# A graph network on one core: the seam of layers 1 and 2, and the last two steps of layer 3, put together anew

## The chip, the cores and the metric

The kernel runs on one core of a Trainium2 chip. The metric is the time of one execution on the device in microseconds (us); three runs of the kernel before gave 2731.63, 2735.09 and 2736.67, median 2735.09. The engines are TensorE (PE; its weight loads are PEld), VectorE (DVE), ScalarE (ACT), GpSimd (POOL) and SyncE (SP), which here only issues DMAs.

## The reference, cut to what matters

Four layers over a graph of N = 4096 nodes with 256 features, all in float32. Each is a residual step with a layer norm behind it:

```python
x = ln(x + attention(x, adj))                    # layer 0: 4 heads, mask adj == 0
x = ln(x + softmax(leaky(es + ed), adj > 0) @ (x @ W1))   # layer 1
d = adj.sum(1) ** -0.5                            # 0 where the sum is 0 (layer 2)
x = ln(x + ((d[:, None] * adj * d[None, :]) @ x) @ W2.T + b2)   # layer 2
x = ln(x + relu((d[:, None] * adj * d[None, :]) @ x @ W3))      # layer 3
```

The change touches the end of layer 1, the start of layer 2, and the end of layer 3, the end of the kernel.

## The kernel before

`xc` holds the rows of x in on-chip memory: 32 chunks of 128 rows. `wh`, a view of the tile `store`, holds layer 1's projected features.

Layer 1 works on 32 units (one chunk of output rows each) in four steps each; `gat_step(t)` runs a pipeline in which the products `attend` (L805) of a step stand six steps behind its scores. Unit u's masks `mk1` (L731) are loaded by SP into buffers of the pool `bias` (`bp`, seven buffers of 4 KB per partition). `finish` (L815, L817, and `ln_stats`, L115 and L116) adds the unit's result onto its chunk and takes mean and variance. The last unit's `finish` waits for the last products of layer 1.

Layers 2 and 3 multiply by the adjacency matrix in the seven-product scheme of Strassen: the matrix is cut in 2 x 2 parts of rows and columns, and the features in 2 x 2 parts as well. One layer is four blocks `jb` of 512 columns in each half, one block 16 steps `c`, so 64 steps a layer and 128 in all (`t`, `n_all`). A step multiplies a pair of chunks p and p + 16:

- `load(t)` (L943): two DMAs of 512 KB from `adjT` into a tile `a`, three steps ahead; four tiles in the pool `l2adj`.
- `sums(t)` (L952, L953, L954): DVE forms five sums and differences of the four parts of `a` into `asum` (two buffers), one step ahead.
- `prepare(p, layer)`: DVE normalizes the two chunks (L124), ACT scales them into `y` (L919; `y` lies in `store`, which layer 1 has left by then), POOL adds the bias `b2` to the chunk in layer 2 (L923), and DVE forms five sums `ysum` (L925, L928, L931). In layer 2's first block the pair p = c + 2 is prepared at the end of step c.
- `Block.product(i, t)` (L983): product i of seven, in the order 0 to 6, added up over the 16 steps in a PSUM bank `m{i}` of its own. Products 2 and 3 take a part of `a` itself as their right side, the other five a part of `asum`.
- after a block, `keep` (L989 on ACT, L991 on DVE) copies the seven banks to `e`; `combine` (L999 to L1008, on DVE) forms the block's four results `hT`; `rows(n)` multiplies them by the weights (L1017, eight row chunks of two halves f each, into the bank `y`) and adds them to `xc` (layer 2: L1026; layer 3: L1031 relu on ACT, then L1032 on DVE) with `ln_stats`. `at_step` spreads this over the steps of the next block, between its products. `block_rstd` (L909 to L911) turns the variances of eight chunks into factors, and `store(h)` normalizes four chunks (L124) and writes them to `out` with one DMA of 512 KB (L1040).

The order on every engine is that of the program (`tc.manual_schedule()`). At the seam it reads:

```python
ln_rstd(0, NCH)            # all 32 chunks: L119 to L121
for t in range(3):
    load(t)
with tc.manual_schedule():
    prepare(0, 0)
    sums(0)
    prepare(1, 0)
```

Behind the last step nothing is left to lie beside: `keep`, then for each half `combine` and four `rows`, then `block_rstd`, then both `store`.

Of the kernel before, what the change touches and what calls it, by code (L numbers as in the profile page):

```python
# [8 lines left out]
F32 = mybir.dt.float32  # L9
BF16 = mybir.dt.bfloat16  # L10
AF = mybir.ActivationFunctionType
# [5 lines left out]
P = 128  # L17
# [27 lines left out]
def tile_gnn(  # L45
# [52 lines left out]
    es_q = keep.tile([P, NA, NBK], F32, name="es_q")  # L98
    pick = keep.tile([P, NA, NA, QB], F32, name="pick")
    ed_b = keep.tile([P, QK], F32, name="ed_b")  # L100
    mid = ExitStack()
    bp = mid.enter_context(tc.tile_pool(name="bias", bufs=7))
    zp = mid.enter_context(tc.tile_pool(name="z", bufs=13))
    ps_q = mid.enter_context(tc.tile_pool(name="ps_q", bufs=1, space=PSUM))
    sc = [ps_q.tile([P, TS], F32, name=f"sc{j}") for j in range(2)]
# [14 lines left out]
        nc.scalar.activation(rstd[:, c0:c1], rstd[:, c0:c1], AF.Sqrt)  # L120
        nc.vector.reciprocal(rstd[:, c0:c1], rstd[:, c0:c1])  # L121

    def ln_apply(dst, src, ci):
        nc.vector.tensor_scalar(  # L124
            dst, src, mv[:, ci, 0:1], rstd[:, ci : ci + 1], ALU.subtract, ALU.mult
        )

# [582 lines left out]

    with ExitStack() as l1:
# [145 lines left out]
        with tc.manual_schedule():  # L861
            for t in range(n_t + NSB + 8):
                gat_step(t)
                if t + 2 < NJ:
                    project_w(t + 2)
                if t + 3 == NJ:
                    take_es(2 * NSB, NBK)
                    spread_es(2 * NSB, NBK, ps_o.tile([P, 512], F32, tag="pm", name="pe"))

                    for j in range(NJ):  # L870
                        nc.sync.dma_start(
                            xc.rearrange("p (a j) e -> p a j e", j=NJ)[:, :, j, :],
                            x0.rearrange("(a j p) e -> p a j e", p=P, j=NJ)[:, :, j, :],
                        )
                    nc.vector.reciprocal(d3, d3)
                    nc.vector.reciprocal(d2, d2)
                    nc.vector.tensor_scalar(sel, sel, -1.0, 1.0, ALU.mult, ALU.add)
                    nc.vector.tensor_tensor(d2, d2, sel, ALU.mult)
# [3 lines left out]

    with ExitStack() as l2:
        big = l2.enter_context(tc.tile_pool(name="l2big", bufs=1))
        ap_ = l2.enter_context(tc.tile_pool(name="l2adj", bufs=4))
        sp_ = l2.enter_context(tc.tile_pool(name="l2sum", bufs=2))
        wk = l2.enter_context(tc.tile_pool(name="l2work", bufs=3))
        ps_m = l2.enter_context(tc.tile_pool(name="l2ps_m", bufs=1, space=PSUM))

        w2_sb = big.tile([P, 2, D], F32, name="w2_sb")  # L890
        nc.scalar.dma_start(w2_sb, w2T.rearrange("(c p) e -> p c e", p=P))
        b2_b = big.tile([P, D], F32, name="b2_b")
        nc.scalar.dma_start(b2_b, b2.partition_broadcast(P))
        w3_sb = big.tile([P, 2, D], F32, name="w3_sb")
        nc.scalar.dma_start(w3_sb, w3.rearrange("(c p) e -> p c e", p=P))

        NP = NCH // 2
        NJB = N // 2 // BJ
        NSJ = BJ // P
        T1 = NJB * NP  # L900
        y = store[:, 0 : 2 * NP * D].rearrange("p (h c e) -> p h c e", h=2, c=NP)
        ysum = big.tile([P, NP, 5, P], F32, name="ysum")
        mv2 = mv.rearrange("p (h c) k -> p h c k", h=2)
        rstd2 = rstd.rearrange("p (h c) -> p h c", h=2)

# [4 lines left out]
            nc.scalar.activation(r, r, AF.Sqrt)  # L910
            nc.vector.reciprocal(r, r)  # L911

        def prepare(p, layer):

            dv = d2 if layer == 0 else d3
            for h in range(2):
                ci = h * NP + p
                ln_apply(xc[:, ci, :], xc[:, ci, :], ci)
                nc.scalar.activation(  # L919
                    y[:, h, p, :], xc[:, ci, :], AF.Copy, scale=dv[:, ci : ci + 1]  # L920
                )
                if layer == 0:
                    nc.gpsimd.tensor_tensor(xc[:, ci, :], xc[:, ci, :], b2_b, ALU.add)  # L923
            s = ysum[:, p, :, :]
            nc.vector.tensor_tensor(  # L925
                s[:, 1:3, :].rearrange("p a d -> p (a d)"), y[:, 0, p, :], y[:, 1, p, :], ALU.subtract
            )
            nc.vector.tensor_tensor(  # L928
                s[:, 3:5, :], y[:, :, p, 0:P], y[:, :, p, P : 2 * P], ALU.add
            )  # L930
            nc.vector.tensor_tensor(  # L931
                s[:, 0, :], y[:, 0, p, 0:P], y[:, 1, p, P : 2 * P], ALU.add
            )

        adj_t = {}
        adj_s = {}

        def load(t):
            jb, c = divmod(t % T1, NP)
            a = ap_.tile([P, 2, 2, BJ], F32, tag="adj", name="a")  # L940
            for k in range(2):
                m0 = (k * NP + c) * P
                nc.sync.dma_start(  # L943
                    a[:, k, :, :],
                    adjT[m0 : m0 + P, :].rearrange("p (h j i) -> p h j i", h=2, i=BJ)[:, :, jb, :],
                )
            adj_t[t] = a

        def sums(t):
            a = adj_t[t]  # L950
            s = sp_.tile([P, 5, BJ], F32, tag="asum", name="asum")
            nc.vector.tensor_tensor(s[:, 4, :], a[:, 0, 0, :], a[:, 1, 1, :], ALU.add)  # L952
            nc.vector.tensor_tensor(s[:, 0:2, :], a[:, 0, :, :], a[:, 1, :, :], ALU.add)  # L953
            nc.vector.tensor_tensor(s[:, 2:4, :], a[:, :, 0, :], a[:, :, 1, :], ALU.subtract)  # L954
            adj_s[t] = s

        class Block:
            def __init__(self, layer, jb):
# [2 lines left out]

            def product(self, i, t):
                c = t % NP
                a, s = adj_t[t], adj_s[t]
                left = (
                    ysum[:, c, 0, :],
                    y[:, 0, c, 0:P],
                    ysum[:, c, 2, :],
                    ysum[:, c, 1, :],
                    y[:, 1, c, P : 2 * P],  # L970
                    ysum[:, c, 3, :],
                    ysum[:, c, 4, :],
                )[i]
                right = (
                    s[:, 4, :],
                    s[:, 1, :],
                    a[:, 0, 0, :],
                    a[:, 1, 1, :],
                    s[:, 0, :],
                    s[:, 2, :],  # L980
                    s[:, 3, :],
                )[i]
                nc.tensor.matmul(self.m[i], left, right, start=(c == 0), stop=(c == NP - 1))  # L983

            def keep(self):
                self.e = wk.tile([P, 7, BJ], F32, tag="e", name="e", bufs=1)
                for i in range(7):
                    if i % 2 == 0:
                        nc.scalar.copy(self.e[:, i, :], self.m[i])  # L989
                    else:  # L990
                        nc.vector.tensor_copy(self.e[:, i, :], self.m[i])  # L991
# [15 lines left out]
                    tt(o, o, e[2], ALU.add)  # L1007
                    tt(o, o, e[5], ALU.subtract)  # L1008

            def rows(self, n, tag="y"):  # L1010

                h, s = divmod(n, NSJ)
                ci = h * NP + self.jb * NSJ + s
                w = w2_sb if self.layer == 0 else w3_sb
                py = ps_m.tile([P, 512], F32, tag=tag, name="py")
                for f in range(2):
                    nc.tensor.matmul(  # L1017
                        py[:, 0:D],
                        self.hT[:, h, f, s * P : (s + 1) * P],
                        w[:, f, :],  # L1020
                        start=(f == 0),
                        stop=(f == 1),
                    )
                row = xc[:, ci, :]
                if self.layer == 0:
                    nc.vector.scalar_tensor_tensor(  # L1026
# [2 lines left out]
                else:  # L1029
                    r = wk.tile([P, D], F32, tag="relu", name="relu")  # L1030
                    nc.scalar.activation(r, py[:, 0:D], AF.Relu, scale=d3[:, ci : ci + 1])  # L1031
                    nc.vector.tensor_tensor(row, row, r, ALU.add)  # L1032
                ln_stats(wk, row, ci)

            def store(self, h):
                ob = wk.tile([P, NSJ, D], F32, tag="ob", name="ob", bufs=2)
# [14 lines left out]
                f(*args)  # L1051

        n_all = 2 * T1
        ln_rstd(0, NCH)
        for t in range(3):
            load(t)
        with tc.manual_schedule():
            prepare(0, 0)
            sums(0)
            prepare(1, 0)  # L1060
            blk = None
            for t in range(n_all):
                layer, tl = divmod(t, T1)
                jb, c = divmod(tl, NP)
                if c == 0:
                    blk = Block(layer, jb)
                if t + 3 < n_all:
                    load(t + 3)
                if t + 1 < n_all:
                    sums(t + 1)  # L1070
                for i in range(7):
                    blk.product(i, t)
                    if i == 2:
                        do(t, "mid")
                del adj_t[t], adj_s[t]
                if layer == 0 and jb == 0 and c + 2 < NP:
                    prepare(c + 2, 0)
                do(t, "end")
                if c == NP - 1:
                    blk.keep()  # L1080
                    if t == n_all - 1:
                        break
                    at_step(t + 1, "mid", blk.combine, 0)
                    at_step(t + 2, "mid", blk.combine, 1)
                    for n in range(2 * NSJ):
# [8 lines left out]
                    if layer == 1:  # L1094
                        for h in range(2):
                            at_step(t + 3 + NSJ + h, "end", blk.store, h)
            for h in range(2):
                blk.combine(h)
                for n in range(h * NSJ, (h + 1) * NSJ):
                    blk.rows(n, f"m{n % 7}")  # L1100
            block_rstd(NJB - 1)
            for h in range(2):
                blk.store(h)


# [49 lines left out]
```

## Time and profile before

| | us |
|---|---|
| runs: lowest, median, highest | 2731.63, 2735.09, 2736.67 |
| the profiled execution, its span | 2734.35, 2732.6 |
| layer 1's last product ends | 1875.29 |
| layer 2's first product starts | 1881.54 |
| layer 3's last seven-product step starts, ends | 2699.2, 2705.2 |
| PE's last product ends | 2723.0 |

The span is counted from the first to the last instruction; the profiled execution's own time is 1.75 us longer. The mean granted clock of TensorE over the span is 0.992 of full speed. A line such as `L983 PE` names the line of the kernel and the engine; in the chain of waits a row holds its start, its length and what ran or was waited for.

### The profile page before, as it was taken

The numbers are of one execution on the slowest core, as the hardware profiler recorded it, in microseconds if no ns is written. First come the engines' busy times: TensorE is split into PE (matmuls) and PEld (weight loads), VectorE is DVE, ScalarE is ACT, GpSimd is POOL, SyncE is SP. The second block draws the span as 40 slices with busy tenths as digits, with TensorE's granted clock in tenths as the row PEclk, the third lists the DMA queues.
The fourth block names the chain that finished last, engine by engine and source line by source line (L and its number), as shares of the span: only waits on it lengthen the run. The fifth ranks groups of instructions, "written<-read, shape, count | busy, mean of one in ns | idle before, by whom it ended". The sixth has DMA issues, their size and how long they took to land.

```text
span 2732.6 us, 58953 instructions
## 1 busy us (share of the span) xinstructions
PE 2677.8 (98%) x23824; PEld 1836.4 (67%) x23824; DVE 2183.5 (80%) x3995; ACT 1647.8 (60%) x2675; POOL 379.4 (14%) x660
## 2 busy tenths in 40 slices
PE   8999999999999999999979999999999999999997
PEld 4777777777777777777768888885444444444443
DVE  4999999999999989999758888885866577676575
ACT  2899999999999999999857777771100001000000
POOL 1222232222222222223200000001200000000000
PEclk9999999999999999999999999999999999999998
DMA  6444444444444444444452222204554554555552
GB/s 146 94 96 96 89 94 95 92 96 94 88 96 95 92 90 96 97 89 91 143 160 73 77 78 77 74 20 133 179 159 155 174 159 153 168 175 161 183 174 69
DMA packets 679489, 312.35 MB, mean 114 GB/s; under 512 B 553520, under 2 KB 583600, under 8 KB 679216
## 3 DMA queue, kind: packets, MB, share of 16 engines
q1 hardware_dynamic: 655776, 265.10, 39.5%
q0 software_dynamic: 21632, 42.05, 4.3%
q8 instruction: 186, 3.05, 0.5%
q10 hardware_dynamic: 1808, 1.44, 0.2%
q14 instruction: 87, 0.71, 0.1%
HBM read 262.41 MB, written 46.07 MB: 113 GB/s over the span
## 4 chain that ended last, share of the span: by engine, by line
PE 94%; DVE 2%; DMA 2%; issue 1%; ACT 1%; SPq 0%; POOL 0%; DVEq 0%; POOLq 0%; ACTq 0%
PE m L983 28%; PE po L431 17%; PE sc L374 16%; PE po L805 16%; PE ptr L413 11%; PE py L1017 2%; PE pp L343 1%; PE pq L321 1%; PE pv L232 1%; PE pk L212 1%; DMA xt<-in_xT 0%; DMA mk<-edge 0%; DMA norm<-lt 0%; DMA x<-xs 0%; SPq L731 0%
## 5 line engine op out<-in xcount | busy, mean ns | idle before, releaser
L383 DVE CUSTOM_DVE_ANT_0 z<-sc,bias 128x1024 f32<-128x1024 f32 x512 | 606.0, 1221 | 50.9 <-PE sc L374 50.8
L399 ACT ACTIVATE z<-z,nm 128x1024 f32<-128x1024 f32 x512 | 590.6, 1154 | 0.0
L421 ACT COPY pt<-ptr 128x1024 f32<-128x1024 f32 x507 | 510.3, 1007 | 66.5 <-PE ptr L413 65.4
L431 PE MATMUL po<-pt,xc 128*64 128x128 f32 x8192 | 504.0, 276 | 0.0
L374 PE MATMUL sc<-store,qT 64*128 64x512 f32 x2048 | 502.9, 604 | 0.1
L805 PE MATMUL po<-store,pt 128*128 128x257 f32 x2048 | 447.2, 380 | 12.6 <-issue 12.6
L431 PEld LDWEIGHTS po<-pt,xc 128*64 128x64 f32 x8192 | 442.1, 137 | 17.5 <-DVE pt L419 0.2
L413 PEld LDWEIGHTS ptr<-ident,z 64*128 64x128 f32 x8192 | 322.9, 138 | 181.0 <-issue 86.9
L805 PEld LDWEIGHTS po<-store,pt 128*128 128x128 f32 x2048 | 389.1, 190 | 70.5 <-issue 12.7
L983 PE MATMUL m<-asum,ysum 128*128 128x512 f32 x768 | 356.7, 594 | 6.3 <-issue 6.3
L413 PE MATMUL ptr<-ident,z 64*128 64x64 f32 x8192 | 356.7, 225 | 5.1 <-ACT pt L421 3.7
L374 PEld LDWEIGHTS sc<-store,qT 64*128 64x128 f32 x2048 | 193.9, 189 | 115.6 <-issue 109.5
L983 PEld LDWEIGHTS m<-asum,ysum 128*128 128x128 f32 x768 | 146.2, 191 | 177.7 <-issue 160.8
L983 PE MATMUL m<-asum,store 128*128 128x512 f32 x512 | 263.3, 596 | 0.0
L983 PE MATMUL m<-a,ysum 128*128 128x512 f32 x512 | 246.0, 594 | 0.0
L989 ACT COPY e<-m 128x512 f32<-128x512 f32 x32 | 18.5, 585 | 351.3 <-PE m L983 351.3
L301 POOL DMA_DIRECT2D edge<-mk x256 | 143.1, 559 | 558.8 <-ACT mk L295 541.8
L759 ACT ACTIVATE z<-z,es_q 128x1024 f32<-128x1024 f32 x128 | 146.6, 1145 | 120.4 <-DVE mx L746 112.0
L952 DVE TENSOR_TENSOR asum<-a 128x512 f32<-128x512 f32 x128 | 88.0, 688 | 163.9 <-PE m L983 163.9
L284 DVE SCALAR_TENSOR_TENSOR bias<-rt,gb,u 128x512 f32<-128x512 f32 x256 | 194.2, 759 | 9.1
L795 DVE STREAM_TRANSPOSE pt<-z 128x1024 f32<-128x1024 f32 x128 | 158.0, 1236 | 41.7 <-PE po L805 41.7
L983 PEld LDWEIGHTS m<-asum,store 128*128 128x128 f32 x512 | 97.9, 191 | 123.2 <-issue 121.3
(122 smaller groups left out, 2601.3 us busy)
## 6 DMA issues: line engine op xcount, KB each, us to landing
a<-in_adjT SPq DMA_DIRECT2D x256, 512.0 KB, 5.1
raw<-in_adjT SPq DMA_DIRECT2D x512, 128.0 KB, 3.9
edge<-mk POOLq DMA_DIRECT2D x256, 128.0 KB, 2.4
mk<-edge SPq DMA_DIRECT2D x256, 128.0 KB, 2.9
xt<-in_xT SPq DMA_DIRECT2D x8, 512.0 KB, 5.1
xq<-in_xT SPq DMA_DIRECT2D x32, 128.0 KB, 3.6
xr<-in_x SPq DMA_DIRECT2D x32, 128.0 KB, 3.0
rb<-norm POOLq DMA_DIRECT2D x128, 32.0 KB, 2.4
```

The source lines that it names most:

```text
L284: nc.vector.scalar_tensor_tensor(self.bias[k][:, m0 : m0 + HT], rt, gb, u, ALU.mult, ALU.add)
L301: nc.gpsimd.dma_start(edge[self.ib * P : (self.ib + 1) * P, k * TS + m0 : k * TS + m0 + HT], mk)
L374: nc.tensor.matmul(ps[j][:, q * 512 : (q + 1) * 512], self.rows.qT[j * HD : (j + 1) * HD, self.pr, :], kT[j * HD : (j + 1) * HD, self.pr, ...
L383: nc.vector.tensor_tensor_reduce(z, ps[j], self.rows.bias[k], 1.0, NEG, ALU.add, ALU.max, self.mx[:, j, k : k + 1],)
L399: nc.scalar.activation(z, z, AF.Exp, bias=self.nm[:, j : j + 1], accum_out=self.ls[:, j, k : k + 1],)
L413: nc.tensor.transpose(pa[:, r, c, :], z[half, c * P : (c + 1) * P], ident[half, half])
L421: nc.scalar.copy(to, pa)
L431: nc.tensor.matmul(self.po[j * HD : (j + 1) * HD, 0:P], v_sb[:, ci, h * HD : (h + 1) * HD], self.pt[j][k][:, c, :], start=(ci == 0), stop= ...
L759: nc.scalar.activation(self.z[s], self.z[s], AF.Prelu, bias=self.eq[:, s : s + 1], alpha=SLOPE)
L795: nc.vector.transpose(self.pt[:, :, s, :], self.z[s].rearrange("p (b r) -> p b r", r=QB))
L805: nc.tensor.matmul(self.po[:, 0 : D + 1], self.pt[:, b, :, :].rearrange("p s i -> p (s i)"), wh[:, b, :], start=(b == 0), stop=(b == NBK - 1),
L983: nc.tensor.matmul(self.m[i], left, right, start=(c == 0), stop=(c == NP - 1))
```

## The change

Five things are done.

1. Of layer 2's work, the pairs 0 and 1 (`NE = 2`) are prepared in `gat_step`'s loop, at step n_t + 6, behind the end of unit 30 and ahead of the end of unit 31. For that the factors of chunks 0 to 30 are formed there and that of chunk 31 alone later; `y` and `ysum` of these pairs lie in tiles of their own (`y_e`, `ysum_e`), and the weights and `b2` are loaded by SP in step 12 of layer 1, no longer by ACT at the seam.
2. The adjacency tile is cut in two tiles of half the size, which take the seven buffers of the pool `bias`; the first three loads stand in the last steps of layer 1. In layers 2 and 3 a load now stands behind the second product of a step.
3. `sums` writes its last two differences with two instructions of 512 elements instead of one of 1024. Ahead of the loop it stands before anything that waits for chunk 31.
4. The products of a step run in the order 2, 3, 0, 1, 4, 5, 6, and the PSUM pool waits tile by tile for what lay there before.
5. The last two steps are put together in `Block.end`: each product for both steps, one after the other; four banks are copied by ACT and three are read by DVE from PSUM; the rows' products stand between; the additions stand on POOL, but two on DVE; normalizing and writing are done half by half, in four DMAs of 256 KB, the last of them on ACT's queue, and one of the last four normalizations on POOL.

```diff
+    def load_last_weights():
+        nc.sync.dma_start(w2_sb, ...)
+        nc.sync.dma_start(b2_b, ...)
+        nc.sync.dma_start(w3_sb, ...)
     def load(t):
-        a = ap_.tile([P, 2, 2, BJ], F32, tag="adj", name="a")
         for k in range(2):
+            a = bp.tile([P, 2, BJ], F32, tag="bias", name=f"a{k}")
...
             for t in range(n_t + NSB + 8):
                 gat_step(t)
+                if t == NJ + NSB:
+                    load_last_weights()
+                if n_t <= t < n_t + 3:
+                    load(t - n_t)
+                if t == n_t + NSB + 2:
+                    ln_rstd(0, NCH - 1)
+                    for p in range(NE):
+                        prepare(p, 0)
...
-            nc.vector.tensor_tensor(s[:, 2:4, :], a[:, :, 0, :], a[:, :, 1, :], ALU.subtract)
+            nc.vector.tensor_tensor(s[:, 2, :], a0[:, 0, :], a0[:, 1, :], ALU.subtract)
+            nc.vector.tensor_tensor(s[:, 3, :], a1[:, 0, :], a1[:, 1, :], ALU.subtract)
...
-        ln_rstd(0, NCH)
-        for t in range(3):
-            load(t)
         with tc.manual_schedule():
-            prepare(0, 0)
             sums(0)
-            prepare(1, 0)
+            ln_rstd(NCH - 1, NCH)
...
-                for i in range(7):
+                if t >= n_all - 2:
+                    if t == n_all - 1:
+                        blk.end(t - 1)
+                    continue
+                for n, i in enumerate(order):
                     blk.product(i, t)
+                    if n == 1 and t + 3 < n_all:
+                        load(t + 3)
```

`Block.end`, cut to its order:

```python
def products(i):                 # both steps
    for t in (t0, t0 + 1):
        self.product(i, t)
    if i in (0, 2, 3, 4):
        nc.scalar.copy(e[:, i, :], m[i])
def onto_x(n):                   # relu on ACT, then the addition
    nc.scalar.activation(r, py[n][:, 0:D], AF.Relu, scale=...)
    eng = nc.vector if n > NSJ and n % 2 else nc.gpsimd
    eng.tensor_tensor(xc[:, ci, :], xc[:, ci, :], r, ALU.add)
...
products(2); products(4); products(0); products(3)
tt(hT[:, 0, 1, :], e2, e4, ALU.add)
tt(o0, e0, e4, ALU.subtract)
tt(o1, e0, e2, ALU.add)
tt(o0, o0, e3, ALU.subtract)
products(6)
tt(hT[:, 0, 0, :], o0, m[6], ALU.add)
products(1)
tt(hT[:, 1, 0, :], m[1], e3, ALU.subtract)
tt(o1, o1, m[1], ALU.subtract)
weigh(0, "m2"); weigh(1, "m4")
products(5)
tt(hT[:, 1, 1, :], o1, m[5], ALU.subtract)
weigh(2, "m0"); weigh(3, "m3")
for n in range(4):
    onto_x(n); stats(n)
for n in range(4, 8):
    weigh(n, ..., (0,))          # first halves
put(0, [nc.vector] * 4)          # factors, normalize, two DMAs
for n in (4, 6):
    for i in (n, n + 1):
        weigh(i, None, (1,)); onto_x(i)
    stats(n); stats(n + 1)
put(1, [nc.vector] * 3 + [nc.gpsimd])
```

## The prediction

> **What bounds the kernel now.** I read the page first, then the chain of waits at the two places that the diff touches, then the waits of TensorE, the granted clock by microsecond, and single groups.
>
> ```profile
> PE 2677.8 (98%) x23824; PEld 1836.4 (67%) x23824; DVE 2183.5 (80%) x3995; ACT 1647.8 (60%) x2675; POOL 379.4 (14%) x660
> PE 94%; DVE 2%; DMA 2%; issue 1%; ACT 1%; SPq 0%; POOL 0%; DVEq 0%; POOLq 0%; ACTq 0%
> ```
>
> PE is busy 98% of the span and is 94% of the chain. So only time in which PE is idle or slow can be won, and the diff adds no product and removes none. The chain at the seam:
>
> ```profile
> 1799.85 75.44 PE po L805 x347
> ...
> 1875.51 0.49 DVE xc L817
> ...
> 1876.92 0.24 ACT rstd L120
> ...
> 1878.99 2.55 issue
> 1881.54 18.61 PE m L983 x38
> ```
>
> The last product of layer 1 ends at 1875.29, the first of layer 2 starts at 1881.54: 6.25 us in which DVE normalizes, prepares chunk 0 and sums the first adjacency tile. Then the end:
>
> ```profile
> 2705.14 0.69 DVE hT L999
> ...
> 2707.47 4.73 PE py L1017 x12
> ...
> 2714.88 0.57 DVE hT L1004
> ...
> 2717.57 4.59 PE py L1017 x10
> ...
> 2724.82 0.18 DVE rstd L909
> ```
>
> After the last product (2705.2) DVE and PE take turns; the span ends at 2732.6. The clock, with columns start:end, length, busy time of PE, PEld, DVE, ACT, POOL, clock, DMA share, GB/s:
>
> ```profile
> 1882.00:1883.00 1.00, 1.00 (x2) 0.30 (x2) 1.00 (x2) 0.00 (x0) 0.00 (x0) 0.50 0.00 0
> 2307.00:2308.00 1.00, 1.00 (x2) 0.34 (x1) 0.93 (x4) 0.00 (x0) 0.00 (x0) 0.50 0.00 0
> 2710.00:2711.00 1.00, 1.00 (x3) 0.76 (x3) 0.74 (x3) 0.09 (x1) 0.00 (x0) 0.50 0.00 0
> ```
>
> And a line of PE's waits:
>
> ```profile
> PE py L1017 <- DVE xc L1026: 2.1, 1, 2.1
> ```
>
> Behind each idle stretch products run at half clock for about 3.4 us, so a gap costs some 1.7 us more than itself. The wait at L1026 is the one stall between the seam and the end: in layer 2, at 2302, PE waits 2.1 us for a late DVE.
>
> **The change part by part.** A logical product of 512 columns issues in 0.86 us (two records, 0.43 each), so a step of seven takes 6.01; a row chunk of L1017 (two halves) takes 0.86.
>
> *Seam.* Before: last attend 1875.29; step 1 of layer 2 begins at 1889.69 (the timeline's group of six records at 1887.97, four of them step 0's). That is 14.4 us for a 6.01 us step: 6.25 idle, 2.1 clock.
>
> After, the statistics of 31 chunks and the preparation of pairs 0 and 1 stand on DVE behind unit 30's end (1862.8), where DVE now idles 12.54 us for L815. They need 0.85 (1876.71 to 1877.55) and twice 3.0 (1883.53 to 1886.55), so are done near 1869.7, with 5.6 us to spare; ACT and POOL idle there too. If that cover failed, up to 3 us would come back. Loads 0 to 2 stand behind the last mask loads on SP as before, but write ring buffers that DVE frees earlier: landed long before. In the built order the first product waits for pair 0's first difference and the first adjacency tile, not for unit 31's end. So products 2 and 3 run from 1875.3 to 1877.1 at full clock. DVE first does unit 31 (1875.31 to 1876.7), then the sums. Product 0 needs the first (0.69): 1877.42. Product 1 needs the second (starts 0.6 later, 1.22 long): 1878.55. Then 4, 5, 6 back to back: step 1 starts at 1882.0. Gain 7.7 us; two bubbles of 0.3 and 0.3 remain. For the five preset waits ahead of the first product I take off 0.05.
>
> Here a rule stands against the trace. The row: PE idle 2.14 us at 2302 lost the clock at 2305.8; idle 1.51 us at 1412.9 kept it. The Trainium skill, "TensorE: Matmul & The Clock Gate", What's actually happening, says the clock falls after an idle window of about 3.4 us. By the rule the 2.1 us gaps would cost nothing beyond themselves; by the row each costs 1.7. I take the row. For my bubbles (0.6 in all) both say no fall; were the point lower than 1.5 us, seam gain would be 6.0.
>
> *Steps 0 to 14.* Splitting L954 (1218 ns for 1024 elements, starts 1.13 apart) into two of the L952 kind (688 ns, starts 0.60 apart) adds 0.07 to DVE's step: 5.89 becomes 5.96 against PE's 6.01. DVE starts step 1's sums at 1880.5, and product 0 wants them at 1883.7, so the cover is 2 us and does not shrink. Cost 0. Elsewhere DVE waits 2 to 3 us a step for PE. In the stall at 2302 DVE has no reserve: two sums more, 0.15 us lost.
>
> *Weights on SP.* Three DMAs (640 KB) stand between mask loads of units 3 and 4, instead of on ACT at 1853.5, when it idled. At the 350 GB/s that windows with a DMA share near 1 show, 2 us; masks are loaded over three units ahead, and only unit 4's and later stand behind the three (they wait for memory of layer 0, free by then). Taken 0, range 0 to 1.
>
> *Order of products and the ring.* Seven buffers of half a step replace four of a step. A load's second half now waits for product 2 of the step that it follows by three: S+1.1 us instead of S-2.6 (S is that step's start). The sums that need it start at S+12.2. Landing:
>
> ```profile
> DMA to landing us min/median/max: 4.0/5.1/10.6
> ```
>
> 11.1 us cover even the longest, which was at the seam's burst. SP's stores of `out` hold loads behind them as before. Cost 0.
>
> *End.* Zero is the start of step 126 (2693.18). Before, the span ends at 39.42. After, PE runs pairs of products: 2, 4, 0, 3, 6, 1 take 12 × 0.86 = 10.31; rows 0, 1 to 12.03; product 5 to 13.75; rows 2, 3 to 15.46; then four first and four second halves to 18.9. I checked each for its operand: sums of step 127 reach the second result at 2.0, wanted at 2.58; product 6 ends at 8.59, its sum (0.69, PSUM in) at 9.5, wanted at 10.31; product 1's at 11.2; product 5 ends 13.75, hT at 14.65, wanted at 17.18. No gap: PE ends at 18.9 instead of 29.8 (2723.0), at full clock.
>
> DVE takes statistics 0 to 3 behind hT: 14.65; with 0.65 each and POOL's additions (L923: 815 ns, against 421 on DVE in L1032) the fourth ends at 17.85. Root with ACT 0.75, four L124 at 0.33: 19.9. ACT's root stands ahead of relu 4, so relu 4 to 7 run 18.35 to 20.3. Rows 4 to 7: addition and two statistics, twice, end at 23.4 on DVE; root 0.7; three L124 to 25.1, the fourth on POOL by 25.2. Out: before, data flow ended 1.7 us ahead of the span's end and began 1.0 after the first issue; 512 KB instead of 1 MB are left, 1.5 us at 345 GB/s: end at 29.0.
>
> POOL's fourth normalization has no row there. Bounds: 0.41 (DVE's own) and 1.6 (twice L923); taken 0.8. And POOL beside DVE costs DVE:
>
> ```profile
> L928 DVE TENSOR_TENSOR ysum<-store x32: 417/680/946, 1879.6 to 2352.8; 128x256 f32<-128x256 f32 x32
> ```
>
> This addition takes 417 ns in layer 3, where POOL is idle, and 946 in layer 2 beside L923. The Trainium skill, "SBUF — State Buffer", section SBUF: two separate sides, says a DVE instruction with two SBUF inputs and a POOL one lock each other out for a whole instruction. The end has two such DVE additions (rows 5 and 7), one of them beside POOL: by the row 0.53, by the rule up to 0.8 if both meet in the worst phase. I take 0.6. Gain at the end 39.4 − 29.6 = 9.8; bounds 7.5 (all of POOL slow, one clock fall) and 10.6.
>
> **Sum.** 7.65 + 9.8 − 0.15 = 17.3 us. The profiled execution took 2734.35 (span 2732.6 and 1.75 around it), 0.74 under the median of the three runs. 2734.35 − 17.3 = 2717.05; against the median 2735.09 − 17.3 = 2717.8, which I give.
>
> **The rivals.**
>
> *Half the gain.* A wait takes the place of the removed ones: if the first product did wait for unit 31 and the sums, PE would start at 1877.4 and lose the clock: 3.0 us less. If POOL's chain runs late by one addition per pair of rows, the end loses 2 to 3. Together 11 to 12: 2723.5. For it: POOL in the end has no row. Against: operands stand in time, above.
>
> *The ring starves (slower).* One mechanism: a half tile later than 11.1 us delays DVE's sums and PE in each of some 120 steps. From 0.15 us a step the 17.3 are gone; a landing of 11.6 us, 0.5 a step, gives 2735 − 17.3 + 60 = 2778. Against: median 5.1, share of DMA 0.5 in these stages.
>
> *It doesn't do what it says.* The sums could stay last and PE idle as before at the seam: only the end's 9.8 is left, 2725.3.
>
> **How the numbers follow.** Forecast 0.70 (2714 to 2721, from the bounds above and the runs' own 5 us), half 0.18, no gain at the seam 0.05, ring 0.04, small losses that eat it all 0.03. A measurement of this kernel tells about 0.2%, 5.5 us, from no change. Faster by more: the first three cases but for a few of their worst, 0.91; same 0.05; slower 0.04. Range 2711.5 to 2724.5: the bounds below, and most of the half case above.
>
> **What would show it.** Seam: PE idle under 1 us between L864 and L1009 of the changed kernel, clock 1.00, step 1 some 6.7 us behind the last attend. Steps: 6.01 each, L973 waiting for PE, not for DMA. End: no PE gap between the last products and rows, clock 1.00, PE done 18.9 us after step 126 starts, the span 10.7 us later. It is wrong if PE waits for adjacency DMAs, if the clock falls at the seam, or if POOL's additions hold the statistics back by more than 1 us.

## The result, and the profile after

| | before | after | ratio, 95% interval |
|---|---|---|---|
| first series: median of 6 runs each (lowest, highest) | 2734.89 (2731.63, 2736.67) | 2719.44 (2715.12, 2722.1) | 0.9944 (0.9931 to 0.9957) |
| the changed kernel repeated: 9 runs before, 5 after | 2733.11 (2732.57, 2735.74) | 2715.06 (2714.02, 2718.9) | 0.9933 (0.992 to 0.9947) |

The changed kernel is faster by 15.45 us in one series and by 18.05 in the other; 17.3 was forecast. The profiled executions have spans of 2732.6 and 2716.8 us.

First the page of after: busy time by engine, and shares of the chain.

```profile
PE 2672.4 (98%) x23824; PEld 1831.6 (67%) x23824; DVE 2187.9 (81%) x4117; ACT 1648.4 (61%) x2677; POOL 386.3 (14%) x667
PE 95%; DMA 1%; DVE 1%; issue 1%; ACT 1%; SPq 0%; POOL 0%; POOLq 0%; ACTq 0%; DVEq 0%
```

PE has the same 23824 matmuls, is busy 5.4 us less (they run less time at half clock), and DVE's share of the chain falls from 2% to 1%. Next PE's timeline at the seam (start, length, instruction, and in brackets the idle time and what ended it; L864 is `attend`, L1009 the seven-product step):

```profile
1876.62 1.90 PE L864 MATMUL po<-store,pt 128*128 128x257 f32 x8
1878.36 1.88 PE L1009 MATMUL m<-a,ysum_e 128*128 128x512 f32 x4
1880.80 1.10 PE L1009 MATMUL m<-asum,ysum_e 128*128 128x512 f32 x2 [0.56 <-DVE asum L973]
1881.93 1.95 PE L1009 MATMUL m<-asum,y_e 128*128 128x512 f32 x4
1883.73 1.88 PE L1009 MATMUL m<-asum,ysum_e 128*128 128x512 f32 x4
1885.44 1.88 PE L1009 MATMUL m<-a,ysum_e 128*128 128x512 f32 x4
```

Products 2 and 3 follow the last attend (ends 1878.52) without a gap. Only product 0 waits, 0.56 us for the first sum, and product 1 some 0.3. Step 1 starts at 1885.44, 6.92 us behind the last attend; before it was 14.42. The clock holds through both bubbles, as the windows of after show (start:end, length, busy time of PE, PEld, DVE, ACT, POOL, clock, DMA share, GB/s); the last two cut the end in the time of the products and the time behind them:

```profile
1881.00:1882.00 1.00, 0.96 (x3) 0.16 (x2) 1.00 (x2) 0.00 (x0) 0.00 (x0) 1.00 0.00 0
1882.00:1883.00 1.00, 1.00 (x3) 0.52 (x4) 1.00 (x3) 0.00 (x0) 0.00 (x0) 1.00 0.00 0
...
2687.40:2706.50 19.10, 19.10 (x61) 11.21 (x59) 11.64 (x24) 5.38 (x12) 3.40 (x5) 1.00 0.00 0
2706.50:2716.80 10.30, 0.03 (x1) 0.00 (x0) 5.74 (x18) 0.85 (x3) 2.43 (x3) 0.75 0.30 102
```

From the start of step 126 PE works 19.1 us without a gap at full clock, and 10.3 us follow. The chain of waits of after at the end tells what those are made of:

```profile
2701.34 1.74 PE py L1040 x8
...
2703.72 0.73 POOL xc L1094
...
2704.47 0.44 DVE bnst L116
...
2706.00 0.72 POOL xc L1094
...
2706.81 0.72 POOL xc L1094
2707.53 3.98 issue
2711.51 1.46 POOLq L1255
```

POOL's additions (L1094) and DVE's statistics take turns. The 3.98 us put down to "issue" hide work: the timeline of DVE has additions, statistics and factors of rows 4 to 7 in them, and normalizing starts at 2711.51.

To compare kernels I cut each profile at three marks that all of them have: the end of the last attend, the start of step 1 of layer 2, the start of step 126.

| profile | span | last attend ends | seam, to step 1 | middle, to step 126 | end, to the span's end |
|---|---|---|---|---|---|
| before | 2732.6 | 1875.27 | 14.42 | 803.49 | 39.42 |
| after | 2716.8 | 1878.52 | 6.92 | 802.0 | 29.36 |

The three stages give 7.5, 1.5 and 10.06: 19.05 us. 3.25 of them are missing in the span, because layer 1 ended later. The experiments ask what each stage's gain consists of, where the 1.5 come from, and whether the 3.25 belong to the change.

### The profile page after: what moved, and what is told of

Its sections match the earlier page's. It is cut to its first block, busy times and chain, and to the rows that moved or that the text cites. A ratio compares the mean times of both kernels' runs of the same rounds, so it can differ in the third digit from the quotient of the medians.

```text
span 2716.8 us, 59024 instructions
## 1 busy us (share of the span) xinstructions
PE 2672.4 (98%) x23824; PEld 1831.6 (67%) x23824; DVE 2187.9 (81%) x4117; ACT 1648.4 (61%) x2677; POOL 386.3 (14%) x667
## 3 DMA queue, kind: packets, MB, share of 16 engines
q10 hardware_dynamic: 1392, 1.05, 0.1%
## 4 chain that ended last, share of the span: by engine, by line
PE 95%; DMA 1%; DVE 1%; issue 1%; ACT 1%; SPq 0%; POOL 0%; POOLq 0%; ACTq 0%; DVEq 0%
PE m L1009 28%; PE po L432 18%; PE sc L375 17%; PE po L864 16%; PE ptr L414 11%; PE py L1040 2%; PE pp L344 1%; PE pq L322 1%; PE pk L213 1%; PE pv L233 1%; DMA mk<-edge 1%; PE sc L140 0%; DMA bqk_sb<-in_bqk 0%; DMA xt<-in_xT 0%; SPq L263 0%
## 5 line engine op out<-in xcount | busy, mean ns | idle before, releaser
L864 PE MATMUL po<-store,pt 128*128 128x257 f32 x2048 | 447.3, 380 | 12.6 <-issue 12.6
L864 PEld LDWEIGHTS po<-store,pt 128*128 128x128 f32 x2048 | 388.7, 190 | 70.9 <-issue 12.7
L1009 PE MATMUL m<-asum,ysum 128*128 128x512 f32 x672 | 324.7, 592 | 0.0
L1009 PEld LDWEIGHTS m<-asum,ysum 128*128 128x128 f32 x672 | 127.7, 190 | 160.3 <-issue 141.1
L973 DVE TENSOR_TENSOR asum<-a,a 128x512 f32<-128x512 f32 x128 | 88.0, 688 | 156.9 <-PE m L1009 156.9
L1009 PE MATMUL m<-asum,store 128*128 128x512 f32 x448 | 210.5, 592 | 0.0
L1009 PE MATMUL m<-a,ysum 128*128 128x512 f32 x448 | 210.5, 592 | 0.0
L279 DVE STREAM_TRANSPOSE rt<-raw 128x512 f32<-128x512 f32 x256 | 179.9, 703 | 0.3 <-issue 0.3
```

What stands on the lines that cost most here:

```text
L279: nc.vector.transpose(rt.rearrange("p (b r) -> p b r", r=QB), self.raw_now[:, half * nb : (half + 1) * nb, :],)
L864: nc.tensor.matmul(self.po[:, 0 : D + 1], self.pt[:, b, :, :].rearrange("p s i -> p (s i)"), wh[:, b, :], start=(b == 0), stop=(b == NBK - 1),
```

## The experiments

**One part at a time.** `seam_only` keeps the old end:

```diff
-                if t >= n_all - 2:
-                    if t == n_all - 1:
-                        blk.end(t - 1)
-                    continue
...
+            for h in range(2):
+                blk.combine(h)
+                for n in range(h * NSJ, (h + 1) * NSJ):
+                    blk.rows(n, f"m{n % 7}")
+            block_rstd(NJB - 1)
+            for h in range(2):
+                blk.store(h)
```

> The changed kernel, with the last two steps of layer 3 as in the kernel before (step by step, then keep, combine, rows, block_rstd, store). Theory (the gain is 7.5 us of the seam and 10 us of the end, and they add): from the last attend product to the start of layer 2's step 1 6.9 us as in the changed kernel, from the start of step 126 to the span's end 39.4 us as before; the time falls by 7.5 us against before, near 2727.4. Rival (the weights on SP and the moved tiles lengthen layers 0 and 1 by some 3 us, which the changed profile shows as a last attend at 1878.5 instead of 1875.3): the last attend at 1878 again, and the time only 4 us lower.

`end_only` takes the early preparation out of layer 1's loop, puts the weights back on ACT's queue, and keeps the order of products and the waits tile by tile:

```diff
-                if t == NJ + NSB:
-                    load_last_weights()
-                if n_t <= t < n_t + 3:
-                    load(t - n_t)
-                if t == n_t + NSB + 2:
-                    ln_rstd(0, NCH - 1)
-                    for p in range(NE):
-                        prepare(p, 0)
...
+        load_last_weights()
+        ln_rstd(0, NCH)
+        for t in range(3):
+            load(t)
         with tc.manual_schedule():
+            prepare(0, 0)
             sums(0)
-            ln_rstd(NCH - 1, NCH)
+            prepare(1, 0)
```

> The changed kernel with the seam as before: no early preparation, weights on ACT, all factors, three loads, prepare 0, sums 0 and prepare 1 behind layer 1. The order of products, the PSUM waits by tile, the ring and the end stay as changed. Theory: the end takes 29.4 us from the start of step 126; at the seam products 2 and 3 can start when pair 0's first difference is there, 4.4 us behind the last attend instead of 6.25, but at half clock, and step 1 starts 12 to 13.5 us behind it instead of 14.4. The time falls by 11 to 12 us. Rival of the moved weights: the last attend stands near 1875 here and near 1878 in the run with the seam alone; if start-up chance moves it, the two scatter without order.

Measured, five runs each, beside before at 2734.85: `seam_only` 2725.75, ratio 0.9968 (0.9955 to 0.998), gain 9.1; `end_only` 2725.81, ratio 0.9964 (0.9951 to 0.9978), gain 9.0. Both missed what was expected: 7.5 for `seam_only`, 11 to 12 for `end_only`. By stages, `seam_only` has seam 6.92, middle 802.0, end 38.0; `end_only` 13.5, 802.0 and 29.4. The parts don't disturb each other: the seam of `seam_only` and the end of `end_only` are those of after. What the expectations left out are the 1.5 us of the middle, which both have, and in `seam_only` an end 1.4 shorter than in before, by one loss of the clock less (the last section says when it is lost). The profiled execution of `end_only`, 2722.24, lies 12.1 us under that of before, as its stages give (12.5, less 0.3 for a later last attend); its five runs lie 5 us apart, and the median is one of three late ones. PE's timeline of `end_only` shows what early preparation is for:

```profile
1873.70 1.90 PE L864 MATMUL po<-store,pt 128*128 128x257 f32 x8
1880.00 3.78 PE L1001 MATMUL m<-a,ysum_e 128*128 128x512 f32 x4 [4.40 <-DVE ysum_e L749]
```

With the new order of products but late preparation, PE still waits 4.4 us for the pair's sums and loses the clock (four records in 3.78 us, not 1.88): only 0.8 of the seam is won (14.33, the mean of before, against 13.5).

**The order of products.** `order_0_6` has all of the change but for this:

```diff
-        order = (2, 3, 0, 1, 4, 5, 6)
+        order = (0, 1, 2, 3, 4, 5, 6)
...
-                    if n == 1 and t + 3 < n_all:
+                    if n == 3 and t + 3 < n_all:
```

> The changed kernel with the products in the order 0 to 6, and the load behind product 3. Theory (the order is worth what products 2 and 3 cover of unit 31's end and the first sum): PE idles 2.1 us behind the last attend, step 1 starts 8.4 us behind it at full clock, 10.1 if the clock falls. Nothing else changes: step 6.01, end 29.4. Rival (the early preparation alone makes the seam gain): still 6.9.

One run: 2720.62; seam 10.24, middle 802.0, end 29.4. Its timeline and its windows at the seam:

```profile
1879.57 1.16 PE L1009 MATMUL m<-asum,ysum_e 128*128 128x512 f32 x2 [2.34 <-issue]
1880.65 2.04 PE L1009 MATMUL m<-asum,y_e 128*128 128x512 f32 x2
```

```profile
1879.00:1881.00 2.00, 1.43 (x3) 0.68 (x4) 2.00 (x3) 0.00 (x0) 0.00 (x0) 0.87 0.00 0
1881.00:1883.00 2.00, 2.00 (x3) 0.79 (x3) 1.73 (x6) 0.20 (x1) 0.00 (x0) 0.50 0.00 0
```

PE idles 2.34 us and then works at half clock. The view names no releaser; by DVE's timeline the sum that product 0 takes (L973) ends at 1879.36, 0.2 ahead of it. The order is worth 10.24 − 6.92 = 3.3 us here, half of it idle time and half clock. The rival, that early preparation alone makes the gain, asked for 6.9.

**Waits of PSUM tile by tile.** In `pool_waits` the first product waits for everything that lay in layer 1's PSUM pool:

```diff
-            tc.tile_pool(name="l2ps_m", bufs=1, space=PSUM, reuse_waits="tile")
+            tc.tile_pool(name="l2ps_m", bufs=1, space=PSUM)
```

> The changed kernel without the PSUM waits tile by tile: the first product then waits for unit 31's addition onto its chunk. Theory (the later waits for the sums hide it): products 2 and 3 start 0.7 us later and the two bubbles behind them close, step 1 starts 6.8 to 6.9 us behind the last attend, no loss. Rival of the prediction (a wait of the first product costs 3 us): 9 us or more.

PE's timeline of `pool_waits`:

```profile
1876.07 1.95 PE L1009 MATMUL m<-a,ysum_e 128*128 128x512 f32 x4 [0.83 <-PE po L864]
1877.86 1.02 PE L1009 MATMUL m<-asum,ysum_e 128*128 128x512 f32 x2
1878.72 1.89 PE L1009 MATMUL m<-asum,y_e 128*128 128x512 f32 x4
```

One run: 2715.33. The first product starts 0.83 us late, and the seam is 6.92 us long all the same. The delay eats the bubbles: DVE's sums decide when products 0 and 1 run, whenever 2 and 3 ran. So the waits tile by tile, taken by themselves, are worth nothing here; DVE's chain behind the last attend sets the seam.

**What sets the seam then.** `sums_early` lets DVE form three of the first tile's five sums behind the early preparation, in tiles that layer 1 no longer uses:

```diff
                     for p in range(NE):
                         prepare(p, 0)
+                    a0, a1 = adj_t[0]
+                    nc.vector.tensor_tensor(s4_first, a0[:, 0, :], a1[:, 1, :], ALU.add)
+                    nc.vector.tensor_tensor(s01_first, a0, a1, ALU.add)
```

`sums(0)` then forms only the two differences.

> The changed kernel with the first two sums of step 0 on DVE behind the early preparation, ahead of unit 31's end, into two tiles that layer 1 has left (pick and ed_b). Theory (the 0.9 us that the seam still costs above a step of 6.01 is DVE doing unit 31's end before the sums): step 1 starts 6.05 us behind the last attend instead of 6.92. Rival (the gap is the first product's own waits, five ahead of it on PE): 6.6 or more.

One run: 2714.78. PE's timeline of `sums_early`:

```profile
1875.65 1.88 PE L1018 MATMUL m<-a,ysum_e 128*128 128x512 f32 x4
1877.36 1.02 PE L1018 MATMUL m<-pick,ysum_e 128*128 128x512 f32 x2
1878.22 1.88 PE L1018 MATMUL m<-ed_b,y_e 128*128 128x512 f32 x4
1879.94 1.88 PE L1018 MATMUL m<-asum,ysum_e 128*128 128x512 f32 x4
1881.66 1.88 PE L1018 MATMUL m<-a,ysum_e 128*128 128x512 f32 x4
```

No bubble is left. Step 1 starts 5.85 us behind the last attend (6.05 expected), 1.07 less than in after: this is the last that the seam has to give.

**POOL at the end.** `end_dve` gives POOL's work there back to DVE:

```diff
-                    eng = nc.vector if n > NSJ and n % 2 else nc.gpsimd
+                    eng = nc.vector
...
-                put(1, [nc.vector] * (NSJ - 1) + [nc.gpsimd])
+                put(1, [nc.vector] * NSJ)
```

> The changed kernel with every addition and normalization of the last two steps on DVE, none on POOL. Theory (POOL's additions run beside DVE's statistics and save DVE time): the six additions cost DVE 0.34 to 0.42 us each, four of them before the first half's factors, and the first half's factors start 0.9 us later; DVE's four L125 of the first half, which take 2.20 us beside POOL, take 1.4 again; in all the span ends 30.0 to 30.6 us after the start of step 126, against 29.4. Rival (POOL, twice as slow per addition, holds the statistics back): 29.4 or less.

One run: 2717.71, end 29.6: 0.2 more than after, where 30.0 or more was expected, and 29.4 or less by the rival. Both missed. The 0.2 stand out all the same: the seven profiles with the end of after agree to 0.02. First what POOL costs DVE: the timeline of DVE in after, and behind it that in `end_dve`:

```profile
2705.81 2.20 DVE L125 TENSOR_SCALAR ob<-xc,mv,rstd 128x256 f32<-128x256 f32 x4
```

```profile
2705.63 1.38 DVE L125 TENSOR_SCALAR ob<-xc,mv,rstd 128x256 f32<-128x256 f32 x4
```

The four normalizations of the first half take 0.82 us more while POOL adds rows 4 and 6 (2706.00 to 2707.53): two of the four take 0.82 and 0.81 instead of 0.41 each, the others stay as they were. The groups of after from 2700 on give the prices (count, busy us, mean ns of one, idle before):

```profile
L1094 POOL TENSOR_TENSOR xc<-xc,relu 128x256 f32<-128x256 f32 x6 | 4.4, 744 | 736.5 <-ACT relu L1092 736.2
L125 DVE TENSOR_SCALAR ob<-xc,mv,rstd 128x256 f32<-128x256 f32 x7 | 3.4, 546 | 0.1
L116 DVE BATCH_NORM_STATS2 bnst<-xc 128x6 f32<-128x256 f32 x8 | 3.3, 412 | 0.7 <-POOL xc L1094 0.7
L125 POOL TENSOR_SCALAR ob<-xc,mv,rstd 128x256 f32<-128x256 f32 x1 | 1.4, 1392 | 4.0 <-DVE rstd L122 4.0
L1094 DVE TENSOR_TENSOR xc<-xc,relu 128x256 f32<-128x256 f32 x2 | 0.8, 402 | 0.0
```

POOL takes 744 ns for an addition that DVE does in 402, and 1392 for a normalization that DVE does in 406 when alone (in `end_dve`). The seven instructions moved are worth 2.6 us of DVE's time, counted from start to start in `end_dve` (1.61 and 0.67 for four and two additions, 0.33 for the normalization; by their lengths it would be 2.8, but they overlap). Of these 0.82 come back in the slower L125 of the first half and 0.16 in those of the second, beside POOL's own (1.22 us for three, against 1.06), 0.7 as waits of the statistics for POOL, and 0.24 because POOL's normalization ends behind DVE's last (2712.97 against 2712.73). That leaves 0.7. Next the issue of the last write on ACT's queue, in the timeline of after and then of `end_dve`:

```profile
2713.00 0.40 ACTq L1108 DMA_DIRECT2D out_x<-ob  x1
```

```profile
2712.58 0.40 ACTq L1108 DMA_DIRECT2D out_x<-ob  x1
```

Counted from the start of step 126 (2687.44 and 2686.34) these are 25.56 and 26.24, which is 0.68 apart. From there to the span's end it is 3.8 us in after and 3.35 in `end_dve`, for the same 512 KB in the last two writes; so 0.2 are left in the end. The write itself is not the reason: it lands 2.36 us behind its issue in after and 2.26 in `end_dve`. The rest lies behind the landing, in the engines' closing `DRAIN` instructions; here are POOL's in after and then in `end_dve`, in the view of their line (shortest, median and longest in ns, first and last start):

```profile
L1255 POOLq DRAIN  x3: 40/93/4498, 2711.5 to 2716.5; - x3
```

```profile
L1255 POOLq DRAIN  x2: 40/71/102, 2715.4 to 2715.7; - x2
```

In after POOL has one more, which begins with its normalization at 2711.5 and lasts to 2716.0, 3.0 us behind the end of that normalization and 0.3 behind the last `DRAIN` of SP. All seven profiles with a normalization of POOL at the end have it, and the six without have none. So this one instruction saves DVE 0.33, gives back 0.16 and 0.24, and then costs 0.3 more: I would estimate from these numbers that after gains some 0.4 us with it on DVE and the additions left on POOL. That was not run.

**The middle, and layers 0 and 1.** 1.5 us of the middle and the 3.25 of layer 1 called for repetitions. `before_a`, `before_b` and `before_c` are the kernel before, unchanged, one run each (2736.89, 2735.32 and 2735.19, beside a fourth of 2738.18); `after_again` is the changed kernel (five runs, in the first table).

> The kernel before, once more, for the scatter of its stages. Of the profiled difference 1.5 us stand between step 1 and step 126: before lost the clock behind the 2.14 us stall at 2304, the changed kernel kept it in seven profiles. Theory (chance of the phase, as at 1326, where six of ten profiles lost it): some of these three keep it, and then have 802 us there instead of 803.5; in the end, with two such gaps, 38.0 or 39.4. Rival (the new order keeps the clock): all three lose it, 803.5.

> The changed kernel once more, for the scatter. Theory: the seam 6.92 and the end 29.4 to within 0.1, from step 1 to step 126 802.0 or 803.6 (clock kept or lost behind the stall), and the last attend anywhere from 1875 to 1879, by the first DMAs and the clock behind the idle time near 1326. Rival (the change itself delays layers 0 and 1): the last attend at 1878 to 1879 again, with the early part of layer 0 as in the kernel before.

The stall at 2302, in the timeline of after:

```profile
2300.07 1.13 PE L1040 MATMUL py<-w_sb,hT 128*128 128x256 f32 x4 [2.34 <-DVE xc L1057]
```

All four profiles of before idle 2.13 to 2.14 us there, lose the clock behind it, and have a middle of 803.48 to 803.49. All eight of after and of the kernels above idle longer, 2.34 or 2.35, keep it, and have 801.99 to 802.0. So what was expected of `before_a` to `before_c`, that some keep it, did not come. But position does decide, and no part of the change as such. In every profile the clock changes only at times that lie whole multiples of 3.413 us apart (the last section has the figures). Cut along these times, the stall of before lies in one window and that of after in two, first before, then after:

```profile
2302.12:2305.54 3.42, 1.43 (x6) 1.09 (x7) 3.10 (x8) 0.47 (x2) 0.00 (x0) 1.00 0.61 193
2305.54:2308.95 3.41, 3.41 (x6) 1.35 (x5) 2.87 (x8) 0.43 (x2) 0.00 (x0) 0.50 0.00 0
```

```profile
2295.22:2298.64 3.42, 2.51 (x6) 0.76 (x4) 3.38 (x6) 0.00 (x0) 0.00 (x0) 1.00 0.37 137
2298.64:2302.05 3.41, 1.98 (x7) 1.40 (x8) 2.65 (x8) 0.91 (x2) 0.00 (x0) 1.00 0.00 0
2302.05:2305.46 3.41, 3.41 (x12) 1.87 (x11) 3.34 (x8) 0.00 (x0) 0.00 (x0) 1.00 0.51 159
```

Before has 1.99 us of idle PE in one window, after 0.91 and 1.43 in two. In the four of before the window that holds the stall has 1.99 to 2.14; in the eight, where an edge cuts the stall, the fuller one has 1.26 to 1.94. The four agree because before loses the clock at the seam: it comes back there on an edge, and the stall begins 416.27 to 416.47 us later, within 0.2 of 122 windows. After keeps the clock at the seam, and in `order_0_6` and `end_only`, which lose it there as well, the stall begins 415.87 and 415.35 us behind its return. The 1.5 us are thus a by-effect and in part luck: `after_again` and `sums_early`, with 1.94 and 1.91, kept the clock by a hair.

Layers 0 and 1 are the opposite case. The last attend ended at 1875.27, 1877.83, 1877.00 and 1876.88 in the four of before, at 1878.52 and 1876.51 in the two of after, and at 1875.24 in `pool_waits`, whose layer 1 is that of after. Two causes can be seen. One is the start: the first scores begin at 23.39 in after, 23.17 in `before_a`, 21.16 in before. The other is an idle stretch near 1326. Here it is in PE's timeline of after, with the window behind it in after and then in `pool_waits`:

```profile
1328.57 0.71 PE L414 MATMUL ptr<-ident,z 64*128 64x64 f32 x16 [2.00 <-ACT pt L422]
```

```profile
1330.00:1340.00 10.00, 10.00 (x132) 6.88 (x130) 6.52 (x16) 7.87 (x11) 2.15 (x5) 0.87 0.34 107
```

```profile
1330.00:1340.00 10.00, 10.00 (x157) 7.51 (x153) 8.24 (x20) 8.99 (x13) 3.93 (x6) 1.00 0.40 128
```

After idled 2.00 us and lost the clock (0.87, 132 products instead of 157); `pool_waits` idled 2.52 and kept it. Again the windows tell the two apart: after has all 2.00 in one, `pool_waits` 1.36 and 1.16 in two. Before itself did both: kept in before and `before_a`, lost in `before_b` and `before_c`. Where it was kept, layer 1 ended by 1875.8 (but for `before_a` with its late start), where it was lost, at 1876.5 to 1878.5. So after's 3.25 us are about 2.2 of start and 1.7 of clock (the price in the last section), less 0.5 of shorter idle time: 3.4. The late start seems to be the clock as well: in after and `before_a`, and in no other profile, it is at half for one window between 17.7 and 22 us; that this alone makes the start late was not shown. Both causes occur without the change and are absent in a kernel with it; I take them for scatter, of a size that the 2.6 us between the two series' gains fit into. `seam_only` (1877.05) and `end_only` (1875.60) by themselves looked like the rival, by which the change delays layers 0 and 1. Over all profiles it has no support: the last attend ends at 1876.7 in the mean of the four of before, and at 1876.9 in that of the eight profiles with the early preparation. Less than about 1 us can't be told this way.

**Both leftovers taken.** `both` is `sums_early` with the preparation of pairs 10 to 15 for layer 3 put later, into steps 69 to 74, away from the stall:

```diff
-                            free = (NJB - 1) * NP + p + NSJ + 2
-                            at_step(max(t + 2 + NSJ + s, free), "end", prepare, p, 1)
+                            free = (NJB - 1) * NP + p + NSJ + 2 + 5 * (p >= 10)
+                            at_step(max(t + 2 + NSJ + s + 2 * (p >= 12), free), "end", prepare, p, 1)
```

> The changed kernel with the first two sums early, and in layer 2's last block the preparations of pairs 10 to 15 for layer 3 moved to steps 69 to 74 (they stood at 64, 65 and 69 to 72, beside the block's copies and combinations). Theory (the 2.34 us stall of PE at 2300 is DVE's queue of preparation, combination and row 0's update): no PE wait on L1057 is left, from step 1 to step 126 799.7 us instead of 802.0, the seam 6.05, in all 3.2 us less than the changed kernel, near 2716. Rival (the work is only moved, and PE waits at steps 69 to 74 instead): 802 again.

The median of five runs is 2714.11 (2713.61 to 2715.68), the ratio to before 0.9929 (0.9917 to 0.9942). No wait of PE for DVE's update of `xc` is left in layer 2; the middle is 799.73 (799.7 expected), the seam 5.85. From the last attend on it takes 834.89 us against 838.29 in `after_again`: 3.4 less. In the time the 3.4 us don't show: `after_again` had 2715.06 in the same series, and the 0.95 us between them lie within the scatter of layers 0 and 1.

## Why the prediction was right, point by point

The forecast, 2717.8, lies between the two series. In the table before is the mean of four profiles, after of two.

| term | forecast | measured, before − after |
|---|---|---|
| seam | 7.65 | 14.33 − 6.92 = 7.4 |
| middle | −0.15 | 803.49 − 802.0 = 1.5 |
| end | 9.8 | 39.09 − 29.37 = 9.7 |
| sum | 17.3 | 18.6 |

That both times lie so near to the forecast is in part luck: the middle gave 1.65 us more than its term, and layer 1, which no term has, took 3.25 in the first profile.

*Seam.* The step held: products 2 and 3 follow the last attend, product 0 starts 2.28 us behind it (2.13 forecast), product 1 3.41 (3.26), two bubbles, no fall of the clock. Early preparation cost nothing on the path. In the rival "half the gain" the part on the seam was mispriced: a first product that waits for what lay in layer 1's pool was to cost 3.0, and the nearest thing that was run, `pool_waits`, with a wait of 0.83, cost 0. The products that wait go into the same bubbles. A first product as late as that rival's was not run with early preparation.

*Middle.* The stall grew by 0.2 us as the step said, from 2.14 to 2.34, but the step took it for granted that the clock would go on falling behind it. It was kept in eight profiles of eight. This is the term that was wrong, with 1.65 us the largest error of the sum. The rule weighed in the prediction, that the clock falls behind about 3.4 us of idle time (the Trainium skill, "TensorE: Matmul & The Clock Gate", What's actually happening), would have priced this stall right in after, and wrong in before, where 2.14 lost the clock four times of four. The row that I preferred was right of before and wrong of after. Both ask how long PE is idle; what told the two apart is how much of that lies in one window of 3.413 us, as the last section has it.

*Weights on SP and the ring.* Both cost 0 as far as can be told, as taken. A line of the loads of after (L764), in the view of that line:

```profile
DMA to landing us min/median/max: 4.0/4.7/7.4
```

The longest landing fell from 10.6 to 7.4 us, against 11.1 us of cover, and PE and DVE wait for no adjacency tile. The starving ring fell by this, and "doesn't do what it says" by the seam.

*End.* PE was done 19.1 us after step 126 starts (18.9 forecast), and the span ended 10.3 later (10.7). The total was right to 0.1, but the POOL term was wrong in kind. It took 0.6 for two-input additions of DVE beside POOL; those took 402 ns, but nothing of POOL ran beside them (POOL's last addition ends at 2707.53, DVE's first begins at 2707.93), so neither the row nor the rule weighed for them was put to the test. What met POOL were L125, with one tensor and two columns of factors as inputs; two of the four took twice as long: +0.82. Two misses offset this one: the last four statistics stand 0.54 us apart where I took 0.65 (0.4 in all), and POOL's normalization, 1.39 long where I chose 0.8 between 0.41 and 1.6, runs beside three L125 and ends only 0.24 behind them. Normalizing ended at 25.53 behind the start of step 126; 25.2 + 0.6 was forecast. From there to the span's end it took 3.83, as forecast (3.8), but the 0.3 of POOL's long `DRAIN` in it was not foreseen. The rival's POOL that is late by an addition per pair of rows did not come: DVE waited 0.7 in all for POOL, less than the 1 us named as a sign of being wrong.

## What to carry to other kernels

At a seam, put the products first that need nothing of the late operand, prepare their other operand where the slow engine idles, and stop when the late engine's own chain sets the end: shortening waits elsewhere is then worth nothing. Compare profiles stage by stage from a mark that both kernels share; here 3 us of scatter ahead of the mark would have hidden the gains of `sums_early` and `both`, 1 and 3 us. Work moved to a slower engine pays only by what the first one doesn't lose beside it. A stall of about 2 us should be priced twice, with and without the fall of the clock, and shifted code ahead of it can turn the one into the other.

## What the runs showed of the hardware

- The granted clock changes on a grid. In each of the thirteen profiles all its changes lie whole multiples of 3.413 us apart, to 0.003 us: in before it falls at 1878.87, 2305.54 and 2708.31, which is 125 and 118 windows. A fall lasts whole windows (3.41, 6.83, 13.65 or 17.07 us).
- The length of an idle stretch doesn't tell whether the clock is lost behind it: lost behind 2.00 (after), 2.14 (before) and 2.34 (`order_0_6` at the seam), kept behind 2.34 (after), 2.12 (`seam_only` at the end) and 2.52 (`pool_waits`). The idle time of PE in one window does. Behind the first 100 us, 59 windows at full clock have 1.0 us of it or more, those near 1414 left out: the 26 with 1.95 or more were followed by half clock, the 29 with 1.90 or less were not, and of the four between one was. Near 1414, where PE runs products of only 24 columns, two profiles of seven lost it with 1.51; why was not found.
- A loss of one window costs 1.7 us (the middle's 803.49 − 802.0, and the 0.2 by which the stall that keeps the clock is longer), half of 3.41.
- POOL additions slowed DVE's `tensor_scalar` with two columns of factors from 1.38 to 2.20 us for four (two of them took 0.81 to 0.82 instead of 0.41), and left alone the one `bn_stats` that ran beside them for most of its time (at 2703.62: 427 ns, and 427 for the same one in `end_dve`).
- POOL's closing `DRAIN` lasted to 3.0 us past the end of its normalization of 128x256 in all seven profiles that have one (2712.97 to 2716.01 in after).
